# Sparse graph attention with residual and layer norm: the order of own and deep key blocks in a batch's last two tiles, and which engine weighs them

## The chip, the cores and the metric

The kernel runs on one core of a Trainium2 chip. The metric is the device time of one execution in microseconds (us). The engines are named as in the profile: PE is TensorE (PEld its weight loads), DVE is VectorE, ACT is ScalarE, POOL is GpSimd, SP is SyncE. POOL and SP also issue transfers (DMA).

## What is computed

One layer of multi-head attention on a graph, for 16 graphs of 1024 nodes with 512 features and 8 heads of 64, in float32, with a residual and a layer norm. The adjacency is one matrix for all 16 graphs. It is sparse and very uneven: the expected number of neighbours falls with the node's number.

```python
q = (x @ Wq + bq).reshape(b, n, H, HD)
k = (x @ Wk + bk).reshape(b, n, H, HD)
v = (x @ Wv + bv).reshape(b, n, H, HD)
scores = jnp.einsum('bqhd,bkhd->bhqk', q, k) / jnp.sqrt(jnp.float32(HD))
scores = scores + (1.0 - adj)[None, None, :, :] * -1000000000.0
attn = jax.nn.softmax(scores, axis=-1)
out = jnp.einsum('bhqk,bkhd->bqhd', attn, v).reshape(b, n, d)
return _layernorm(x + out @ Wo + bo)
```

## The kernel before

**Tiles and blocks.** The nodes are sorted by their number of neighbours and cut into 8 tiles of 128 queries. A batch (one graph) goes through its tiles in order. Only neighbours are computed: a block holds 128 pairs of a query and a key. In an own block i of a tile, each query of the tile meets its i-th neighbour. OWN (line 27) gives the number of own blocks by tile, 2, 1, 2, 3, 4, 5, 5, 7. Queries with more neighbours than that fill deep blocks, in which each of the 128 lines is a pair of any query of the tile with one more of its neighbours. BLOCKS (line 28) gives their number: one for tile 6, five for tile 7. Tile 1 needs no attention (one key), and tile 0 is done for the first two batches and then in the odd ones, for two batches together. This leaves 34 blocks in batches 0, 1 and the odd ones and 32 in the others, 530 in all.

**What a block does.** POOL gathers the keys' rows of k and v into a tile kvg (gather, line 1230, 512 KB), eight buffers in use (KG_BUFS); for a deep block it also gathers the rows of q into qg (line 1184, 256 KB). An own block uses the tile's q, loaded once by SP (line 1217). DVE multiplies q and k (products, line 1251) and sums by head (scores, line 1255), ACT takes the exponential (exponentials, line 1266). Then the rows of v are weighed by the exponentials (weigh): either ACT does it in eight small instructions, one for each head (line 1276), or DVE in one (line 1280). That frees the kvg buffer. An own block is then added by DVE to the tile's first block (add_own, line 1292; the first block itself, i = 0, needs no addition). A deep block is summed by PE into PSUM (add_up, lines 1301 and 1302), by a matrix that says which line belongs to which query. After the tile's last block, normalise (from line 1304) adds the two, divides, and hands the result to the output product.

**Which engine weighs.** by_act (line 1268) gives the own blocks other than the first to ACT. First and deep blocks go to ACT where the block's number n is even, to DVE where it is odd; in the first half batch all go to ACT, in the last batch all to DVE. Since every batch has an even number of blocks, the pattern is the same in each batch: of the six deep blocks, two go to ACT.

**Beside the blocks.** PE's main work is products: q, k and v of a batch ahead ("fronts"), by a scheme that computes k and v of two tiles together with seven products of sums (lines 947 to 979), and the output product po (line 790) of finished tiles, followed by the residual and the norm on DVE, ACT and POOL (complete, from line 1085) and a scattered store by POOL (line 1125). POOL also gathers x rows for the fronts (line 1001) and for the residual (line 1029).

**What sets the order.** All of it is written by hand: the loop from line 1470 takes one step for each block n, and each engine runs its instructions in the order in which they are issued there. In step n the exponentials of block n + 3 are issued, the products of n + 4, the gathers up to block n + 8, DVE's weighing of n + 1, the addition of own block n, the scores of n + 4, ACT's weighing of n + 2 and PE's sum of deep block n. A tile's normalise comes in the step of the next tile's first block. Between them PE's units of fronts and output products are issued by a credit, which grows in each step by a share of the batch's work. paced (line 1432) scales the share by load_of (line 1424), a guess of DVE's work in the step: 2, one more if DVE weighs block n + 1, one more for an own block that is not the first, and more for a tile's first block.

Of the kernel before, what the change touches and what calls it, by code (L numbers as in the profile page):

```python
# [26 lines left out]
OWN = (2, 1, 2, 3, 4, 5, 5, 7)  # L27
BLOCKS = (0, 0, 0, 0, 0, 0, 1, 5)
# [6 lines left out]
LONE, ONE_KEY, ONE_KEY_AT, ONE_KEY_LAST = 64, 1, (7, 4), (3, 0)  # L35
# [142 lines left out]
def kernel(  # L178
# [37 lines left out]
    B, N, D = x.shape  # L216
# [13 lines left out]
    own = [SHORT_KEYS * t for t in SHORT]  # L230
# [3 lines left out]
    NBT = NB - OWN[ONE_KEY]  # L234
# [19 lines left out]
    with ExitStack() as main:  # L254
# [82 lines left out]
        def merged(b):  # L337
            return b >= PAIRED_FROM and b % 2 == 1

        def tiles_of(b):  # L340
            return [t for t in range(NT) if t or b < PAIRED_FROM or merged(b)]
# [828 lines left out]


        KG, QG, PV, PSUM, QT, RDEN, V1 = {}, {}, {}, {}, {}, {}, {}
        blocks = [(b, t, i) for b in range(B) for t in tiles_of(b) if t != ONE_KEY for i in range(OWN[t] + BLOCKS[t])]
        start = [min(n for n, block in enumerate(blocks) if block[0] == b) for b in range(B)] + [len(blocks)]

        def load_more():
# [90 lines left out]

        def by_act(n):
            b, t, i = blocks[n]
            return 0 < i < OWN[t] or n < total - NBT and (n % 2 == 0 or n < NBT // 2)  # L1270

        def weigh(n):
            v, pv = KG.pop(n), PV[n]
            if by_act(n):
                for h in range(HEADS):
                    nc.scalar.activation(  # L1276
                        pv[:, ts(h, HD)], v[:, ds(D + h * HD, HD)], AF.Copy, scale=pv[:, D + h:D + h + 1]
                    )
                return
            nc.vector.tensor_tensor(  # L1280
                pv[:, 0:D].rearrange("p (h d) -> p h d", d=HD),
                v[:, D:].rearrange("p (h d) -> p h d", d=HD),
                pv[:, D:, None].to_broadcast([P, HEADS, HD]), op=OP.mult,
            )
# [134 lines left out]
        total = len(blocks)  # L1419
# [4 lines left out]
        def load_of(n):  # L1424

            b, t, i = blocks[n]
            had = 2.0 + (not by_act(min(n + 1, total - 1))) + (0 < i < OWN[t])
            if i == 0:
                had += 3.0 if BLOCKS[blocks[n - 1][1]] else 1.3
            return had  # L1430
# [17 lines left out]
        with tc.manual_schedule():  # L1448
# [20 lines left out]
            n = -LEAD_IN  # L1469
            while n < total or plan or rest or urgent or done or finishing or spilled or lone_tiles or not guarded:  # L1470
# [6 lines left out]
                elif n in start:  # L1477

                    b = start.index(n)
                    left = sum(u[0] for u in fronts)  # L1480
# [11 lines left out]
                if 0 <= n + 1 < total and not by_act(n + 1):  # L1492
                    weigh(n + 1)
# [96 lines left out]
```

## Time and profile before

| | |
|---|---|
| time, median of 3 runs | 1903.44 us (1902.83 to 1912.35) |
| the profiled execution's own time | 1892.33 us |
| its span, first to last instruction | 1890.4 us |
| mean granted clock of PE | 0.989 |
| ACT weighing, line 1276 | 3432 instructions, 864.6 us busy |
| DVE weighing, line 1280 | 101 instructions, median 0.683 us |
| DVE product, line 1251, and scores, line 1255 | 530 of each, 0.68 us each |
| DVE own addition, line 1292 | 329 instructions, mean 0.693 us |
| transfers | 544.63 MB, mean 288 GB/s |

How to read what follows. A row of a group or of a timeline names the line of the code, the engine, the operation, and what is written from what, with shapes as partitions x elements. In square brackets, or after the bar, stands the time for which the engine was idle just before, and what ended that. A row of the waits says which instruction waited for which, in total, how often, and the longest. A row of the stretches gives for each engine the busy time and the number of instructions, then the granted clock of PE (1 is full speed), the mean busy share of the 16 DMA engines, and GB/s. Engines run their instructions pipelined, so two instructions in a row can start less than one duration apart.

### The profile page before, as it was taken

The page shows a single profiled execution, that of the slowest core. Times are in us where ns is not written, and L with a number is a line of the kernel's source. Part 1 is how long each engine was busy: PE and PEld are TensorE (multiplying, and loading weights), DVE is VectorE, ACT ScalarE, POOL GpSimd, SP SyncE. Part 2 cuts the span into 40 slices and gives each one's busy share as a digit, 9 for nine tenths or more (in the row PEclk, how much of TensorE's full clock was granted, in tenths as well). Part 3 has the DMA queues.
Part 4 walks back from the last instruction along what each step waited for, and adds up shares of the span by engine and source line. Part 5 has one row for each costly group of instructions (what it writes and reads, how often), then busy time and mean ns, then how long its engine had stood idle before and what let it go on. Part 6 is the DMA issues. An engine that isn't in the chain of part 4 may idle for free. (4 is left out here: it accounts for less than half of the span.)

```text
span 1890.4 us, 25101 instructions
## 1 busy us (share of the span) xinstructions
PE 1815.1 (96%) x5149; PEld 878.2 (46%) x5149; DVE 1700.6 (90%) x3484; ACT 1531.7 (81%) x6016; POOL 1267.4 (67%) x1189
## 2 busy tenths in 40 slices
PE   7989999999999999999999999999999999999995
PEld 3434444444545454444445444444445444444442
DVE  6888889999999999899899989899999999997874
ACT  3627869979888988979798978989898989886794
POOL 1367766777677676757677676767666777656774
PEclk9989999999999999999999999999999999999997
DMA  7357787988889898888889898999889899989993
GB/s 280 114 168 226 233 307 227 315 295 294 308 287 316 305 328 283 305 288 307 312 292 335 271 334 274 314 304 310 301 307 326 293 356 310 314 277 340 334 319 117
DMA packets 188149, 544.63 MB, mean 288 GB/s; under 512 B 32602, under 2 KB 32622, under 8 KB 187986
## 3 DMA queue, kind: packets, MB, share of 16 engines
q0 software_dynamic: 116400, 382.82, 60.6%
q1 hardware_dynamic: 68510, 154.30, 21.8%
q10 hardware_dynamic: 3076, 5.82, 0.9%
q14 instruction: 120, 0.98, 0.2%
q8 instruction: 43, 0.70, 0.1%
HBM read 419.52 MB, written 144.34 MB: 298 GB/s over the span
## 5 line engine op out<-in xcount | busy, mean ns | idle before, releaser
L1276 ACT ACTIVATE pv<-kvg,pv 128x64 f32<-128x64 f32 x3432 | 864.6, 340 | 0.0
L1230 POOL DMA_INDIRECT kvg<-kv_pair,place_row x462 | 526.7, 1140 | 258.0 <-ACT pv L1276 73.3
L790 PE MATMUL po<-wo,oT 128*128 128x512 f32 x816 | 380.1, 596 | 1.0 <-ACT oT L1340 0.9
L790 PE MATMUL pq<-wq,xT 128*128 128x512 f32 x792 | 368.9, 597 | 0.4 <-DVE g L966 0.4
L1255 DVE TENSOR_REDUCE s<-qk 128x8 f32<-128x512 f32 x530 | 360.2, 680 | 7.5
L1251 DVE TENSOR_TENSOR qk<-qt,kvg 128x512 f32<-128x512 f32 x434 | 296.4, 683 | 22.2 <-DMA kvg<-kv_pair,place_row 22.1
L947 PE MATMUL pp<-t,s 128*128 128x512 f32 x504 | 237.4, 593 | 2.7 <-ACT sq_k L800 1.7
L947 PE MATMUL x<-b,xT 128*128 128x512 f32 x504 | 237.8, 594 | 0.8 <-ACT e L960 0.8
L790 PEld LDWEIGHTS po<-wo,oT 128*128 128x128 f32 x816 | 152.6, 191 | 166.8 <-issue 153.9
L1292 DVE TENSOR_TENSOR pv<-pv,pv 128x520 f32<-128x520 f32 x329 | 228.0, 693 | 0.7 <-ACT pv L1276 0.6
L790 PEld LDWEIGHTS pq<-wq,xT 128*128 128x128 f32 x792 | 149.2, 192 | 166.4 <-issue 155.0
L1266 ACT ACTIVATE pv<-s,absent 128x8 f32<-128x8 f32 x434 | 126.3, 293 | 79.8 <-DVE s L1255 76.2
L1001 POOL DMA_INDIRECT x<-in_x_dram,asked_row x120 | 130.2, 1085 | 88.3 <-PE pxT L748 40.5
L1125 POOL DMA_INDIRECT out_dram<-y,asked_row x129 | 144.8, 1122 | 35.7 <-issue 19.8
L800 ACT ACTIVATE sq_k<-kv 128x128 bf16<-128x128 f32 x512 | 150.9, 301 | 6.0 <-DVE kv L970 6.0
L947 PEld LDWEIGHTS pp<-t,s 128*128 128x128 f32 x504 | 94.2, 190 | 114.1 <-issue 101.4
L947 PEld LDWEIGHTS x<-b,xT 128*128 128x128 f32 x504 | 94.3, 191 | 111.5 <-issue 106.5
L1184 POOL DMA_INDIRECT qg<-q_rows,query_row x96 | 106.9, 1114 | 36.5 <-issue 24.7
L947 PE MATMUL z<-b,s 128*128 128x512 f32 x252 | 119.1, 595 | 6.5 <-DVE kv L975 6.5
L1029 POOL DMA_INDIRECT y<-in_x_dram,asked_row x93 | 104.5, 1124 | 27.5 <-issue 25.8
L947 PE MATMUL z<-t,s 128*128 128x512 f32 x252 | 120.0, 599 | 0.0
L947 PE MATMUL pp<-t,xT 128*128 128x512 f32 x252 | 118.4, 592 | 0.0
(276 smaller groups left out, 2766.7 us busy)
## 6 DMA issues: line engine op xcount, KB each, us to landing
kv_pair<-kv SPq DMA_DIRECT2D x98, 512.0 KB
q_rows<-q SPq DMA_DIRECT2D x106, 256.0 KB
qt<-q_rows SPq DMA_DIRECT2D x98, 256.0 KB
residual<-x SPq DMA_DIRECT2D x36, 256.0 KB
y<-residual SPq DMA_DIRECT2D x36, 256.0 KB
kv_rows<-kv SPq DMA_DIRECT2D x15, 512.0 KB
kvg<-kv_pair,place_row POOLq DMA_INDIRECT x462, 6.5
kv_pair<-kv SPq DMA_DIRECT2D x28, 256.0 KB
```

Of the source, the lines that this page charges most:

```text
L790: nc.tensor.matmul(p, lhs(c), w[:, c, :], start=(c == 0), stop=(c == NPAIR - 1))
L800: nc.scalar.activation(sq, s[:, ts(h, P)], AF.Square, scale=scale, accum_out=sums[:, h:h + 1])
L947: nc.tensor.matmul(R[bank], l[:, ts(c, P)], right[:, c, :], start=(first and c == 0), stop=(c == 1), skip_group_check=True,)
L1001: nc.gpsimd.indirect_dma_start(out=y, out_offset=None, in_=x_rows, in_offset=bass.IndirectOffsetOnAxis(ap=asked_row[:, t:t + 1], axis=0), ...
L1125: nc.gpsimd.indirect_dma_start(out=out_rows[b, t], out_offset=bass.IndirectOffsetOnAxis(ap=rows, axis=0), in_=y, in_offset=None, element_o ...
L1184: nc.gpsimd.indirect_dma_start(out=q, out_offset=None, in_=q_rows[b % ROWS], in_offset=bass.IndirectOffsetOnAxis(ap=rows, axis=0))
L1230: nc.gpsimd.indirect_dma_start(out=KG[n], out_offset=None, in_=rows, in_offset=bass.IndirectOffsetOnAxis(ap=(place_row if b else key_row)[ ...
L1251: nc.vector.tensor_tensor(QK[n], q, KG[n][:, 0:D], op=OP.mult)
L1255: nc.vector.tensor_reduce(S[n], QK.pop(n).rearrange("p (h d) -> p h d", d=HD), axis=AX.X, op=OP.add)
L1266: nc.scalar.activation(PV[n][:, D:], S.pop(n), AF.Exp, bias=bias)
L1276: nc.scalar.activation(pv[:, ts(h, HD)], v[:, ds(D + h * HD, HD)], AF.Copy, scale=pv[:, D + h:D + h + 1])
L1292: nc.vector.tensor_tensor(PV[b, t], PV[b, t], pv, op=OP.add)
```

## The change

In batches 1 to 15 the blocks of the tiles with deep blocks (6 and 7) come in another order. Tile 7 runs own 0, own 1, and then deep and own blocks in turn up to the last own block. Tile 6's only deep block comes after its third own block. Blocks keep their number i, and batch 0 keeps its order. Which engine weighs a deep block depends, from batch 1 on, on the parity of b + i and no longer on that of n. In odd batches this gives four of the six deep blocks to ACT, in even ones two. First blocks (i = 0) keep the parity of n, and the rules for the first half batch and for the last batch stay.

```diff
-        blocks = [(b, t, i) for b in range(B) for t in tiles_of(b) if t != ONE_KEY for i in range(OWN[t] + BLOCKS[t])]
+
+        def blocks_of(b, t):
+
+            own, deep = list(range(OWN[t])), list(range(OWN[t], OWN[t] + BLOCKS[t]))
+            if b == 0 or not deep:
+                return own + deep
+            spread = max(1, len(own) // (len(deep) + 1))
+            left = len(own) - spread * len(deep)
+            for j, i in enumerate(deep):
+                own.insert(left + j * (spread + 1), i)
+            return own
+
+        blocks = [(b, t, i) for b in range(B) for t in tiles_of(b) if t != ONE_KEY for i in blocks_of(b, t)]
...
         def by_act(n):
             b, t, i = blocks[n]
-            return 0 < i < OWN[t] or n < total - NBT and (n % 2 == 0 or n < NBT // 2)
+            if 0 < i < OWN[t]:
+                return True
+            turn_of = b + i if b and i else n
+            return n < total - NBT and (turn_of % 2 == 0 or n < NBT // 2)
```

## The prediction

> **What bounds the kernel now.** I read the page's first part, its groups, the waits by engine, stretches of 5 us, and the timelines around the longest PE waits. Part 1 and two of the groups:
>
> ```profile
> PE 1815.1 (96%) x5149; PEld 878.2 (46%) x5149; DVE 1700.6 (90%) x3484; ACT 1531.7 (81%) x6016; POOL 1267.4 (67%) x1189
> ...
> L1276 ACT ACTIVATE pv<-kvg,pv 128x64 f32<-128x64 f32 x3432 | 864.6, 340 | 0.0
> L1230 POOL DMA_INDIRECT kvg<-kv_pair,place_row x462 | 526.7, 1140 | 258.0 <-ACT pv L1276 73.3
> ```
>
> PE is the bound. To see whether its busy time is real I took start-to-start times from its timeline: a 128x512 f32 product is two records, 0.43 us apart, a transpose 0.108 us, one sum (L1301 and L1302) 0.87 us. Counted over the whole timeline this is about 1809 us of PE work in a span of 1890.4 us. The rest is some 25 us of start (to 140 us), 20 to 30 us of end (from 1845 us), and small holes between, of which those over 0.5 us sum to about 43 us. A change that touches no PE work can give back only holes. So I looked for what the largest holes wait for:
>
> ```profile
> POOL kvg L1230 <- ACT pv L1276: 88.0, 72, 6.2
> ...
> POOL kvg L1230 <- DVE pv L1280: 36.2, 16, 4.3
> ...
> DVE qk L1251 <- DMA kvg<-kv_pair,place_row: 25.6, 13, 4.9
> ...
> PE sum L1301 <- DVE pv L1280: 13.8, 6, 3.7
> ```
>
> The columns are total us, times, longest. Numbering the 530 products of L1251 in order gives each DVE wait a block: the waits for kvg of 4.28, 4.87, 4.24 and 2.93 us (804.9, 907.8, 1119.3, 1630.2 us) stand on the first blocks of batches 6, 7, 9 and 14, and nearly all of the 25.6 us lies between the last deep block of a tile 7 and the third tile of the next batch. Four PE waits before a sum follow from them: 3.75, 1.89, 2.82, 2.51 us. How the first comes about, POOL first:
>
> ```profile
> 776.00 0.95 POOL L1184 DMA_INDIRECT qg<-q_rows,query_row  x1 [0.30 <-issue]
> ...
> 790.21 1.01 POOL L1230 DMA_INDIRECT kvg<-kv_pair,place_row  x1 [0.30 <-ACT pv L1276]
> ...
> 796.55 1.01 POOL L1230 DMA_INDIRECT kvg<-kv_pair,place_row  x1 [0.30 <-ACT pv L1276]
> 797.86 1.01 POOL L1230 DMA_INDIRECT kvg<-kv_pair,place_row  x1 [0.31 <-ACT sq_k L800]
> ```
> ```profile
> 804.94 0.69 DVE L1251 TENSOR_TENSOR qk<-qt,kvg 128x512 f32<-128x512 f32 x1 [4.28 <-DMA kvg<-kv_pair,place_row]
> ```
> ```profile
> 806.29 1.22 PE L1301 MATMUL sum<-pv,sums 128*128 128x256 f32 x2 [3.75 <-DVE pv L1280]
> ```
>
> From 776.00 to 791.2 us POOL issues the five deep blocks' pairs of gathers (qg, kvg) and nothing else: 15.2 us, 3.0 us a block. Then come four other jobs, and only at 796.55 the first kvg of batch 6, whose product comes 8.4 us later. By its place in the program this gather belongs to step (7, position 4); DVE passed that step near 786 us. POOL is 10 us behind, then issues a kvg every 1.3 us, 524 KB each, and DMA fills:
>
> ```profile
> 800.00:805.00 5.00, 2.54 (x8) 1.14 (x6) 0.72 (x3) 2.12 (x9) 3.78 (x5) 1.00 1.02 412
> 805.00:810.00 5.00, 3.71 (x8) 2.47 (x9) 4.93 (x9) 2.06 (x9) 2.46 (x3) 0.66 0.97 349
> 905.00:910.00 5.00, 3.11 (x10) 1.48 (x9) 2.20 (x4) 0.47 (x2) 3.78 (x5) 1.00 1.03 400
> 1115.00:1120.00 5.00, 4.11 (x12) 1.90 (x10) 0.72 (x3) 0.00 (x0) 3.78 (x5) 1.00 1.02 411
> 1625.00:1630.00 5.00, 4.09 (x13) 2.10 (x12) 2.04 (x4) 4.06 (x19) 2.52 (x3) 1.00 1.04 411
> ```
>
> The last three columns are clock, DMA share, GB/s. In all four stalls DMA is full at 400 to 412 GB/s while DVE stands still; after the first, PE's clock is 0.66 for 5 us. ACT has its own pattern, summed from its timeline: idle 0 to 1 us in nearly every tile 6, 5% in the own blocks of tile 7, 12% in its deep blocks.
>
> [...]
>
> **The change part by part.** The sum is against the profiled execution: 1892.33 us, of which 1890.4 are span. The median shown is 1903.44, 11.1 more; I carry the difference over unchanged.
>
> (1) *Order of own and deep blocks, batches 1 to 15.* No instruction is added. Tile 7 becomes own 0, 1, then deep and own in turn, ending on an own block; tile 6's one deep block moves from sixth to fourth. DVE's product and reduction, ACT's exponential, both gathers and the sum move with the block. Gathers stay 8 steps ahead until the fronts are used up (7 or 8 for a batch's first block, before and after, worked from the planner's code). POOL: apart from block gathers it issues 129 stores, 120 x, 93 y and small powers, about 0.65 jobs a block at 1.3 us, 0.9 us. A deep block then costs 3.0 + 0.9 = 3.9 us against a pace of 3.33 us per deep block, so POOL falls back by some 3 us in five. Mixed, (5 x 3.0 + 7 x 1.3)/12 + 0.9 = 2.9 us, under the pace of 3.2. DMA: 544.6 MB less the kvg (530 x 0.524) and qg (96 x 0.262) leaves 242 MB, 128 GB/s. A deep run adds 0.786 MB/3.3 us = 238, together 366 GB/s, near the 400 where it is full; mixed, 0.633/3.2 = 198, together 326. Worth: the four PE waits (11.0 us), the shorter waits just behind them (about 4) and two clock dips (5 us at 0.66, and 5 us at 0.71 from 1630: 3.2) make 18. Lateness of POOL also comes from ACT's release of kvg buffers, which stays in part, so I take 60%: -11. Bounds -18 and 0.
>
> (2) *DVE work moved to ACT.* In each of the seven odd batches 1 to 13, four deep blocks instead of two are weighed by ACT; even ones keep two; the last batch keeps DVE. The instruction lists say the same: L1280 101 to 87, L1276 3432 to 3544. DVE: 14 x 0.60 us (start to start) = 8.4 us less. DVE is not the bound, but PE waits for it at pm, z, poT and pxT for some 13 us, half of that in odd batches. I take -2; bounds -7 and 0.
>
> (3) *The same on ACT.* Eight weighings are 1.93 us start to start (771.22 to 773.13 with nothing between), so 3.9 us more per odd batch, 27 in all, at nothing if ACT's idle time covers it. In tiles 6 and 7 of batches 3, 5, 7, 9, 11, 13 that idle time is 6.4, 8.6, 2.8, 4.3, 2.3 and 4.8 us: barely enough in two. Behind a late weighing stand ACT's copies out of PSUM, for which PE waits next, and the release of a kvg buffer, for which POOL waits. Taken +2; bounds 0 and 27.
>
> (4) *Pace of PE's units.* The weights of load_of now alternate (4 and 2 instead of 3 in own blocks), so PE's units come in turns of about 4 and 1 us per step. PE's queue is in order and full, so +1; bounds 0 and +4.
>
> (5) *Edges.* DVE waits 2.9 us in all for L1302 at normalise; the last deep block is now one step earlier, so that goes. At the very end the last block is an own one with ACT's 1.93 us before the add. But DVE waits there for PE's po until 1865.85, which covers it; and five qg are no longer in a row ahead of the 5.47 us wait for POOL at 1839.8. Taken -2; bounds -4 and +2. Tile 7's first sum comes five steps earlier into the single sum buffer, but still two steps after tile 6's normalise: nothing, at most 1.
>
> Sum: -11 - 2 + 2 + 1 - 2 = -12. 1892.3 - 12 = 1880.3 profiled; 1903.4 - 12 = 1891.
>
> **Rivals.** *The holes stay* (0.22). POOL's 124 us of waits for weighings (88.0 + 36.2) say buffers, not the pairs of gathers, make the first kvg late. Then (1) is 0, the rest -1: 1902. Against it: from 776 to 791 us POOL shows only issue gaps of 0.3.
> *ACT becomes the bound in odd batches* (0.16), ending slower: place, tiles 6 and 7 of odd batches; price, 3.9 us each; it decides once less than about half is covered by idle time. Half uncovered is 7 x 1.95 = 14, with +1 of (4) and (1) lost because the next batch's gathers wait on the late weighings, less 4 of (2) and (5): 1914. For it: the two batches with 2.8 and 2.3 us. Against it: any 13 blocks from tile 6 on hold at most 12 for ACT, as before.
> *All middle stalls go* (0.12): -18 - 7 - 4 + 1 = -28, 1875.
> That the change doesn't do what it says is excluded by the instruction lists.
>
> **How the numbers follow.** The forecast, 1891, has 0.50; its own range is 1884 to 1899. The range 1878 to 1908 leaves out about 0.08 of the large gain and 0.12 of the slow case. About 0.5%, 9.5 us, is what a measurement of this kernel can tell from no change. Faster: 0.38 of the forecast and all 0.12. Same: 0.12 of the forecast, 0.20 of the staying holes, 0.03 of the slow case. Slower: 0.13 and 0.02 of the holes.
>
> **What would show it.** Right: DVE's wait for kvg from kv_pair falls from 25.6 us to under 12, and PE's wait for L1280 before a sum in the middle from 11 to under 5; no 5 us at 400 GB/s with DVE under 3; DVE waits for L1302 near 0. Wrong: ACT idle near 0 through odd tiles 7 and waits of DVE or PE for L1276 of several us; or first blocks that still wait for kvg.

## The result and the profile after

| | before | changed | ratio, 95% interval |
|---|---|---|---|
| 16 runs of each: median (range) | 1909.95 us (1900.32 to 1919.07) | 1897.06 us (1890.87 to 1904.53) | 0.9928 (0.9910 to 0.9945) |
| later, another chip, 43 and 4 runs | 1890.40 us (1885.26 to 1900.41) | 1877.85 us (1876.78 to 1879.82) | 0.9943 (0.9923 to 0.9962) |

The changed kernel is faster by 0.6 to 0.7%. The forecast, 1891 over 1903.44, was a ratio of 0.9935. The medians of the same kernel differ by 20 us between the two groups of runs, so below times are compared only as ratios to the kernel before on the same chip, turned into microseconds by 1890 (in experiment 3 by 1927).

The page of the changed kernel, its first part and the two groups that were shown of the kernel before. Lines from 1230 on have moved: the gather of kvg is L1242, the product L1263, ACT's weighing L1291, DVE's L1295, the own addition L1307, the sums L1316 and L1317, the normalised output o L1337, its transpose L1351.

```profile
PE 1816.5 (96%) x5149; PEld 876.6 (46%) x5149; DVE 1695.3 (90%) x3470; ACT 1557.4 (82%) x6128; POOL 1262.6 (67%) x1189
...
L1291 ACT ACTIVATE pv<-kvg,pv 128x64 f32<-128x64 f32 x3544 | 893.4, 340 | 1.8 <-issue 1.8
L1242 POOL DMA_INDIRECT kvg<-kv_pair,place_row x462 | 522.6, 1131 | 258.6 <-issue 94.5
```

ACT has 112 instructions more and 25.7 us more busy time, DVE 14 fewer and 5.3 us less; PE's work is the same. This profiled execution spans 1892.4 us, that of before 1890.4. The latter (1892.33 us) is not one of the 16 runs above, and its DVE shows none of the pauses that no instruction explains ("issue"), which come to 22.5 us in the changed kernel's profile. So their spans can't be subtracted. The waits can be compared, as the second profiles below confirm. DVE's waits of the changed kernel (us in all, times, longest):

```profile
DVE qk L1263 <- DMA kvg<-kv_pair,place_row: 14.3, 13, 2.9
...
DVE pv L1307 <- ACT pv L1291: 8.0, 7, 1.8
```

and PE's:

```profile
PE z L947 <- DVE kv L975: 10.4, 5, 3.9
...
PE poT L1351 <- DVE o L1337: 6.9, 4, 2.5
...
PE sum L1316 <- DVE pv L1295: 4.1, 4, 1.9
```

DVE's wait for kvg fell from 25.6 to 14.3 us and its longest from 4.9 to 2.9. PE's wait for a weighing before a sum fell from 13.8 to 4.1. So far this is what step (1) said. But z, a product that waits for DVE's kv (L975), has come to the top of PE's list, and DVE now waits 8.0 us for ACT's weighings (0.6 before).

For a pair that can be subtracted, both kernels were run and profiled again on one chip, together with the two halves of the change.

### The profile page after: what moved, and what is told of

It reads as the page before. It is cut to its first block, busy times and chain, and to the rows that moved or that the text cites. A ratio compares the mean times of both kernels' runs of the same rounds, so it can differ in the third digit from the quotient of the medians.

```text
span 1892.4 us, 25171 instructions
## 1 busy us (share of the span) xinstructions
PE 1816.5 (96%) x5149; PEld 876.6 (46%) x5149; DVE 1695.3 (90%) x3470; ACT 1557.4 (82%) x6128; POOL 1262.6 (67%) x1189
## 5 line engine op out<-in xcount | busy, mean ns | idle before, releaser
L1291 ACT ACTIVATE pv<-kvg,pv 128x64 f32<-128x64 f32 x3544 | 893.4, 340 | 1.8 <-issue 1.8
L1242 POOL DMA_INDIRECT kvg<-kv_pair,place_row x462 | 522.6, 1131 | 258.6 <-issue 94.5
L1263 DVE TENSOR_TENSOR qk<-qt,kvg 128x512 f32<-128x512 f32 x434 | 296.8, 684 | 13.2 <-DMA kvg<-kv_pair,place_row 13.1
L1307 DVE TENSOR_TENSOR pv<-pv,pv 128x520 f32<-128x520 f32 x329 | 228.4, 694 | 8.2 <-ACT pv L1291 8.0
L947 PE MATMUL z<-b,s 128*128 128x512 f32 x252 | 121.4, 604 | 13.1 <-DVE kv L975 10.4
```

The lines of the kernel that those rows point to most:

```text
L947: nc.tensor.matmul(R[bank], l[:, ts(c, P)], right[:, c, :], start=(first and c == 0), stop=(c == 1), skip_group_check=True,)
L1242: nc.gpsimd.indirect_dma_start(out=KG[n], out_offset=None, in_=rows, in_offset=bass.IndirectOffsetOnAxis(ap=(place_row if b else key_row)[ ...
L1263: nc.vector.tensor_tensor(QK[n], q, KG[n][:, 0:D], op=OP.mult)
L1291: nc.scalar.activation(pv[:, ts(h, HD)], v[:, ds(D + h * HD, HD)], AF.Copy, scale=pv[:, D + h:D + h + 1])
L1307: nc.vector.tensor_tensor(PV[b, t], PV[b, t], pv, op=OP.add)
```

## Experiment 1: both kernels again, and each half alone

The kernel before, unchanged ("before_2"):

> The kernel before once more, unchanged, for a second profile: the one shown before belongs to an execution of 1892 us, 18 us under the median of 16. Both theories: time within 0.2% of before. If the late first gathers of a batch (spreading theory) are what the median execution pays for, this profile, at about 1905 us, shows DVE waiting for kvg from kv_pair for 30 to 45 us, not 25.6, and PE waiting before sums for 15 to 30 us. If the scatter has another source (clock, first batch), these stay at 26 and 14 us.

The changed kernel, unchanged ("after_2"):

> The changed kernel once more, unchanged, for a second profile. Both theories: 13 to 14 us under before. Spreading theory: DVE's wait for kvg from kv_pair is again near 14 us, about half of before's. Smoothing theory (the gain comes from ACT no longer falling behind in a row of own blocks): this wait is no smaller than before's when set beside the second profile of before, and ACT's waits for DVE and DVE's for ACT are.

The new order, with the old engine for each block ("order_alone", an edit to the changed kernel):

```diff
-            turn_of = b + i if b and i else n
+            turn_of = i if b and i else n
```

> The new order of blocks, with the blocks weighed by the engines that had them before (deep blocks 8 and 10 of tile 7 by ACT in every batch, tile 6's by DVE). Spreading theory: the order is what counts, -9 to -12 us of the 13.8, ratio 0.994 to 0.995. Rival, the split counts (DVE is the second busiest engine and is relieved of 14 weighings in odd batches): -3 us or less.

The new split in the old order ("split_alone", an edit to the kernel before):

```diff
-            return 0 < i < OWN[t] or n < total - NBT and (n % 2 == 0 or n < NBT // 2)
+            if 0 < i < OWN[t]:
+                return True
+            turn_of = b + i if b and i else n
+            return n < total - NBT and (turn_of % 2 == 0 or n < NBT // 2)
```

> The old order of blocks, with deep blocks from batch 1 on weighed by the parity of batch plus block number: in odd batches four by ACT instead of two. Spreading theory: between -3 and +3 us, since POOL's five pairs of gathers in a row stay. Rival, the split counts: -6 us or more.

| | ratio, 95% interval | DVE for kvg | PE for a sum's weighing | PE z for kv |
|---|---|---|---|---|
| before_2 | 0.9998 (0.9985 to 1.0010) | 26.4 us | 13.6 us | 6.2 us |
| order_alone | 0.9999 (0.9987 to 1.0010) | 15.7 | 4.2 | 15.5 |
| split_alone | 0.9953 (0.9936 to 0.9969) | 30.5 | 10.6 | 4.2 |
| after_2 | 0.9943 (0.9923 to 0.9962) | 16.1 | 4.9 | 8.0 |

This turns my account over. The new order shortens the waits for kvg and at the sums much as step (1) said, and by itself brings nothing that can be measured: between -2.5 and +1.9 us. The split, which I had put at -2 + 2 = 0, leaves the waits for kvg and most of those at the sums, and by itself brings 8.9 us (6 to 12). Order and split together can't be told from the split alone by these intervals. before_2 shows the same waits as the first profile of before, within about 1 us. Whether a longer execution has more of them wasn't tested, since this one took 1892.7 us, as the first had.

**Where the order's gain went.** The start of batch 14 shows it. In order_alone, DVE's timeline (start, duration, engine and line, and in brackets the idle time before) has:

```profile
1625.91 0.69 DVE L1263 TENSOR_TENSOR qk<-qt,kvg 128x512 f32<-128x512 f32 x1 [2.51 <-DMA kvg<-kv_pair,place_row]
1626.52 0.68 DVE L1295 TENSOR_TENSOR pv<-kvg,pv 128x512 f32<-128x512 f32 x1
1627.13 0.69 DVE L1307 TENSOR_TENSOR pv<-pv,pv 128x520 f32<-128x520 f32 x1
...
1629.85 0.68 DVE L975 TENSOR_TENSOR kv<-z,g 128x512 f32<-128x512 f32 x1
```

PE's timeline, and the two stretches of 5 us around it (PE, PEld, DVE, ACT, POOL with counts; clock, DMA share, GB/s):

```profile
1630.59 2.08 PE L947 MATMUL z<-b,s 128*128 128x512 f32 x2 [5.14 <-DVE kv L975]
```
```profile
1625.00:1630.00 5.00, 0.45 (x2) 0.00 (x0) 4.05 (x10) 5.00 (x22) 3.33 (x4) 0.96 1.01 396
1630.00:1635.00 5.00, 4.41 (x6) 2.19 (x7) 3.01 (x5) 4.33 (x22) 3.78 (x5) 0.50 0.95 371
```

The product still waits 2.51 us for kvg with DMA near full. Behind it in DVE's queue stand a weighing, an own addition, the scores and five small operations, four of them for the products of x, and only then the kv that PE's next product needs. PE does nothing for 5.14 us and then runs at a clock of 0.50. In before_2, kv L975 ran at 1627.12, ahead of the product that waits. Here PE's wait has thus moved from the sum to the next result that PE takes from DVE. That kv now stands behind the product can come from the pace: load_of sees the new order, so order_alone also deals PE's units out to other steps. The two were not separated. Two more long waits for kv appear in order_alone, 3.85 us at 1082.1 and 3.50 at 1194.6; the first is in both profiles of the changed kernel too (3.86 each time), the other two aren't. These two are no returned waits for kvg: in the 10 us before each of them DVE didn't wait for kvg, but had other work ahead of kv, and before_2 already has 2.36 us at the place of the second.

DMA was not relieved either. Of the 342 stretches of 5 us from 140 to 1850 us, DMA moved at least 395 GB/s in 28 of before_2, 30 of split_alone, 34 of the first profile of the changed kernel, and 45 of order_alone and of after_2. In step (1) I had worked out 326 GB/s for a mixed run instead of 366, and had taken the full stretches to go. What went is the long DVE stall inside them.

**What the split does.** The same place in before_2, DVE, PE, and the stretch:

```profile
1630.30 0.69 DVE L1251 TENSOR_TENSOR qk<-qt,kvg 128x512 f32<-128x512 f32 x1 [2.50 <-DMA kvg<-kv_pair,place_row]
1630.91 0.68 DVE L1280 TENSOR_TENSOR pv<-kvg,pv 128x512 f32<-128x512 f32 x1
```
```profile
1631.65 0.70 PE L1301 MATMUL sum<-pv,sums 128*128 128x256 f32 x2 [2.33 <-DVE pv L1280]
```
```profile
1625.00:1630.00 5.00, 4.32 (x14) 2.30 (x13) 2.04 (x4) 4.27 (x20) 3.01 (x3) 1.00 1.04 413
```

and in split_alone, DVE and the stretch:

```profile
1628.08 0.70 DVE L1251 TENSOR_TENSOR qk<-qt,kvg 128x512 f32<-128x512 f32 x1 [3.87 <-DMA kvg<-kv_pair,place_row]
1628.81 0.69 DVE L1255 TENSOR_REDUCE s<-qk 128x8 f32<-128x512 f32 x1
```
```profile
1625.00:1630.00 5.00, 5.00 (x17) 3.04 (x16) 1.89 (x5) 3.18 (x19) 3.45 (x5) 1.00 1.03 417
```

In split_alone DVE waits longer for the same kvg, 3.87 us, and DMA is as full; yet PE is busy for the whole 5 us. The step that issues the product of a batch's first block (n + 4) issues DVE's weighing of block n + 1, which is deep block (7, 9) of the batch before. In the kernel before that weighing stands right behind the product that waits, and PE's sum waits for it. After an odd batch the new split gives (7, 9) to ACT, and the sum doesn't see DVE's stall. Only a few batch starts show such waits. Sums after odd batches (to batches 6 and 14) waited 3.30 + 2.33 = 5.6 us in before_2 and 1.1 in split_alone. Those after even batches, where (7, 9) stays on DVE, waited 5.1 us in before_2 and 6.7 in split_alone. So this wait shrank by 4.5 us, less 1.6 given back after even batches: 2.9 of the 8.9 us. The rest I couldn't pin on one wait.

## Experiment 2: amounts or places

Four edits to the kernel before, run on another chip than experiment 1; the kernel before took 1890.95 us there. "dve_more": in the odd batches 1 to 13, blocks (6, 5) and (7, 9) are weighed twice by DVE, so 14 weighings or 8.4 us more (0.60 us each from start to start).

```diff
-            nc.vector.tensor_tensor(
+            b, t, i = blocks[n]
+            for _ in range(2 if b % 2 and b < B - 1 and (t, i) in ((6, 5), (7, 9)) else 1):
+                nc.vector.tensor_tensor(
...
```

> The kernel before, with two deep blocks of each of the seven odd batches (tile 6's and the third of tile 7, both DVE's) weighed twice by DVE: 14 x 0.60 = 8.4 us more on DVE, nothing else changed, ACT and the pace of PE's units included. Theory now (PE waits for DVE at whatever stands next in its queue, so DVE's work in the tiles of the blocks is paid for one to one): +7 to +10 us, ratio 1.004 to 1.005. Rival, place (the split pays because the last deep block of an odd batch no longer stands behind DVE's product that waits for kvg): 0 to +3. The forecast's own step, that DVE is not the bound and 8.4 us of it are worth 2: +2.

"act_more": in the same batches ACT weighs (7, 8) and (7, 10) twice, 27 us more (14 weighings of 1.93 us).

```diff
-                for h in range(HEADS):
+                b, t, i = blocks[n]
+                for h in [*range(HEADS)] * (2 if b % 2 and b < B - 1 and (t, i) in ((7, 8), (7, 10)) else 1):
```

> The kernel before, with the two deep blocks that ACT weighs in each of the seven odd batches weighed twice by ACT: 14 x 1.93 = 27 us more on ACT, nothing else changed. Theory now: ACT has room, 0 to +3 us. Rival of the forecast, ACT becomes the bound in odd batches: +10 or more. With dve_more it tells what the two halves of the split are worth one by one.

"swap_last": in those batches ACT takes (7, 9) and (7, 11) in place of (7, 8) and (7, 10); the amounts stay.

```diff
-            return 0 < i < OWN[t] or n < total - NBT and (n % 2 == 0 or n < NBT // 2)
+            if 0 < i < OWN[t]:
+                return True
+            if 0 < b < B - 1 and b % 2 and i:
+                return (t, i) in ((7, 9), (7, 11))
+            return n < total - NBT and (n % 2 == 0 or n < NBT // 2)
```

> The kernel before, with ACT weighing the third and the last deep block of tile 7 in odd batches in place of the second and the fourth: as much work on each engine as before, but the last deep block no longer queued on DVE behind the next batch's products. Theory now (amount of DVE's work): -2 to +2 us. Rival, place: -5 us or more.

"split_all": split_alone with the odd batches' pattern in the even ones too, `turn_of = i + 1`. ACT then has four of six deep blocks in every batch from 1 to 14.

> The old order of blocks, with four of six deep blocks weighed by ACT in the even batches 2 to 14 as well: 28 weighings moved from DVE to ACT instead of 14. Theory now: twice the gain of the split, -14 to -18 us against before, as long as ACT's idle time covers 3.9 us per batch. Rival, ACT becomes the bound, or the gain of the split was one of place in odd batches: no more than the split's -9.

| | ratio, 95% interval | in us |
|---|---|---|
| dve_more | 1.0022 (1.0009 to 1.0035) | +4.2 (1.7 to 6.6) for 8.4 us of DVE |
| act_more | 1.0022 (1.0007 to 1.0037) | +4.2 (1.3 to 7.0) for 27 us of ACT |
| swap_last | 0.9966 (0.9951 to 0.9981) | -6.4 (-9.3 to -3.6) for nothing in the amounts |
| split_all | 1.0029 (1.0018 to 1.0040) | +5.5 (3.4 to 7.6) |

DVE's added work is paid by about half, ACT's by about 15%. For dve_more this is less than the +7 to +10 that I expected by then. It is no pure test of the amount either: half of its added weighings are those of (7, 9), in the very place described above, and the sums waited 16.9 us in it instead of 13.6. If work taken away gives what added work costs, which no run tests, the change's amounts come to -4.2 + 4.2 = 0. That is what my -2 + 2 said, with each term about half of what is measured here. So the amounts, as far as these two runs show them, are not what made the split pay. Swapping which two blocks ACT weighs, with no change of amounts, gives 6.4 us, beside split_alone's 8.9 on the other chip. In swap_last's trace the sums after odd batches waited 2.6 us instead of 5.6, those after even ones 6.4 instead of 5.1. The direction is the same as in split_alone, but the net of the two is 1.7 us of the 6.4. So the runs show that this wait moves as described, and not that it makes the gain. swap_last, split_alone and split_all also change what by_act tells load_of, and so the places of PE's units; experiment 3 comes back to that.

In split_all new waits lead. PE's waits there:

```profile
PE z L947 <- DVE kv L975: 12.8, 7, 4.7
PE x L947 <- ACT e L960: 7.1, 2, 4.8
...
PE sum L1304 <- DVE pv L1283: 3.3, 4, 1.7
```

The sums wait 3.3 us only, but PE waits 12.8 us for kv and 7.1 for ACT. Measured against the kernel before on each chip, split_all is some 14 us worse than split_alone. The 7.1 us, of which 4.8 lie in one wait behind ACT's weighings in batch 12, are what the rival "ACT becomes the bound" said. The waits for kv are not: before the two longest, 4.09 us at 439.3 and 4.74 at 663.3, DVE had other work of its own directly ahead of kv. So the rival is real in part, and how much of the 14 us is its doing stays open. In the odd batches alone it shows as DVE's wait for ACT's weighings (0.6 us before, 7.4 and 8.0 after) and doesn't decide.

**A second measure.** PE's work is the same in all these kernels, so I added up PE's busy time times granted clock over the stretches from 140 to 1740 us, which leaves out the start and the last batch. That this product is work done is an estimate. The records of z in order_alone fit it: the four from 1630.59 us on, of which two are shown above, took 3.78 us at a clock of 0.50, four of the same form at 437.72 took 1.98 at 1.00. before_2 had done 1562.7 us of it, after_2 10.0 more, split_alone 4.9 more, swap_last 3.8 more, order_alone 1.0 less, act_more 3.5, split_all 5.7 and dve_more 7.7 less. The signs agree with the measured ratios, and so does the order but for dve_more. The first profile of the changed kernel, the one with the pauses, doesn't fit: it had done 1.4 us less than before_2. PE's idle time in the same stretch is 32.4 us in before_2, 32.6 in order_alone, 29.1 in split_alone and 23.3 in after_2. Single profiles also differ at the end, where the code is the same. Near its last products before_2 ran PE at:

```profile
1860.00:1865.00 5.00, 5.00 (x11) 2.17 (x11) 0.27 (x1) 0.68 (x1) 3.02 (x4) 0.71 0.51 190
...
1870.00:1875.00 5.00, 4.53 (x6) 1.96 (x7) 0.98 (x5) 1.93 (x3) 2.55 (x3) 0.50 0.43 164
```

By the same estimate, clock below 1 cost 6.1 us there after 1830 (busy time times what the clock lacks to 1), 4.5 in the first profile of before, 1.6 in after_2, 1.5 in split_alone, 1.6 in dve_more, 4.6 in act_more, 6.2 in swap_last and nothing in split_all, with the last batch the same in all but after_2. So of the 16.2 us between the spans of before_2 and after_2, some 4.5 are the end's clock by this estimate.

## Experiment 3: the pace, and the gathers of q

These four ran on yet another chip, on which the kernel before took 1927.48 us.

"pace_alone": the kernel before, whose load_of alone is told the new split.

```diff
...
-            had = 2.0 + (not by_act(min(n + 1, total - 1))) + (0 < i < OWN[t])
+            had = 2.0 + (not paced_act(min(n + 1, total - 1))) + (0 < i < OWN[t])
```

> The kernel before, with every block in its place and weighed by the engine that weighed it before; only load_of, by which PE's units are dealt out to the steps, is told the changed split of the deep blocks. Planner theory (the split pays because it moves PE's units, one output product unit from the last batch to the one before among them): -5 to -9 us. Engine theory (it pays because DVE's queue is shorter or has the last deep block no more): -2 to +2.

"split_old_pace": split_alone, whose load_of is told the old split, by the same line. All weighings are as in split_alone, and PE's units are dealt out as before.

> The old order of blocks with the changed split, load_of still told the old one, so that PE's units stand where they stood before. Planner theory: -2 to +2 us. Engine theory: -6 to -9, as split_alone.

"after_flat_pace": the changed kernel with one weight for all blocks of tiles 6 and 7 but the first.

```diff
+            if BLOCKS[t] and i:
+                had = 3.0
```

> The changed kernel, with load_of giving every block after the first of tiles 6 and 7 the same weight, 3, so that PE's units no longer come in turns of 4 and 1 us. If the uneven pace is what eats the gain of the new order: 4 to 10 us under the changed kernel, so 15 to 20 under before. If a stall taken away at a sum comes back at the next result of DVE that PE needs, whatever the pace: within 3 us of the changed kernel, about -10 against before.

"no_qg": the kernel before without the 96 gathers of q; deep blocks multiply with the tile's own q, so their scores are others, with as much work on DVE, ACT and PE.

```diff
-                tag, bufs = ("qt", Q_BUFS) if fronts or i % 2 else ("xT", 4)
-                QG[n] = work.tile([P, D], F32, tag=tag, name=f"qg_{n}", bufs=bufs)
-                gather_q(QG[n], b, (query_row if b else query_row0)[:, g:g + 1])
...
-            if i < OWN[t]:
-                q = QT[b, t] if i < OWN[t] - 1 else QT.pop((b, t))
-            else:
-                q = QG.pop(n)
+            q = QT[b, t] if n + 1 < total and blocks[n + 1][:2] == (b, t) else QT.pop((b, t))
```

> The kernel before, leaving out the 96 gathers of queries for deep blocks (it uses the tile's own queries there, so deep scores are those of other pairs): POOL has 96 jobs of 1.4 us fewer, DMA 25 MB less, five in a row per batch. The forecast's step, POOL and DMA fall behind there and make the next batch's first kvg late: DVE's wait for kvg falls from 26 to under 8 us and the time by 11 to 18. Theory now (PE and DVE are both nearly full and in order, so a wait for kvg that goes comes back as one of DVE for PE or of PE for the next result of DVE): the wait falls, the time by 5 us or less.

| | ratio, 95% interval |
|---|---|
| pace_alone | 0.9996 (0.9974 to 1.0019) |
| split_old_pace | 1.0013 (0.9986 to 1.0041) |
| after_flat_pace | 0.9972 (0.9953 to 0.9990) |
| no_qg | 0.9735 (0.9700 to 0.9770) |

The split's pace told alone costs nothing within 5 us. split_old_pace shows no gain: its interval, -2.7 to +7.9 us, leaves out the -6 to -9 that I expected if the split acts through DVE's queue alone. It fits what I had written for the other case, that the split pays only together with its own pace. But split_alone was not run on this chip, so chip and pace are not separated, and the point stays open. It weakens the account by place: in swap_last, too, the pace went with the place. after_flat_pace is faster than before by 0.28%, some 5 us, less than either of the two cases that I had named; the changed kernel was not run there, so nothing says whether its pace helps or hurts. No version was shown to beat the changed kernel.

no_qg is the plain miss. I had expected 5 us or less and measured 51 on this chip. Some of that may be the chip's pauses (last section), of which no_qg has fewer. Its runs, 1872 to 1878 us, are 12 to 18 us below what the kernel before took on the chip of experiment 1 (1890), where such pauses are absent. DVE's wait for kvg in its profile:

```profile
DVE qk L1245 <- DMA kvg<-kv_pair,place_row: 0.5, 1, 0.5
```

Without the second gather of each pair the waits for kvg are gone. POOL's idle time before the gathers of kvg from kv_pair, where the rival "the holes stay" looked for the cause, is longer there: 328.5 us, of which 109.6 ended with ACT's weighings, against 258.0 and 73.3 in the first profile of before. So the premise of step (1) holds: the pairs make the first kvg late. Whether they do so by POOL's time or by DMA's bytes, no_qg doesn't separate, since it takes away both. What they cost is larger than my 5 us, and by the 12 to 18 us may be what step (1) had put on it (18 at most); the 51 can't be told from the pauses. Spreading the pairs doesn't collect it.

## Why the prediction was right in number and wrong in its sum

- **Step (1), -11 for the order: the step that failed.** What it said of the waits was right: 25.6 to 14.3 us for kvg, 13.8 to 4.1 for the sums, no wait for kvg of 4 us left. That DMA would be relieved was wrong (45 full stretches against 28). Its price was wrong, 0 (-2.5 to +1.9) in place of -11. (A small part was a slip: the two clock dips counted 3.2 us, though PE was busy for only 3.71 and 3.40 of their 5 us, which makes 2.2. That the dips would go with the waits was an estimate; in after_2 the clock was 0.58 in the stretch in which z's wait of 3.86 us for kv ended.) I priced the waits that go and asked too little what is late next: PE's waits on z for kv came to 15.5 us in order_alone against 6.2, about as much more as the sums lost (9.4). At batch 14 kv stands further back in the same delayed DVE queue; the other two long waits come from where PE's units and DVE's other work now stand.
- **Steps (2) and (3), -2 and +2 for the split.** The net of the amounts, 0, fits dve_more and act_more (4.2 and 4.2), if taking away gives what adding costs. But the split is worth -8.9. swap_last shows with equal amounts that it matters which weighings are moved, together with the pace that goes with them; I had treated all 14 alike. A wait that accounts for it is seen for 2.9 of the 8.9 us, the one at the sums. Whether the rest needs the split's pace is open (split_old_pace).
- **Step (4), +1 for the pace.** pace_alone tells load_of only the new split, not the new order: -0.8 (-5.0 to +3.7). That is no contradiction, but the pace of the whole change was not run alone.
- **Step (5), -2 at the edges.** DVE's wait for L1302 at normalise went from 2.9 us to 0.5 for L1317. The end itself varies by up to 6 us with the clock (the estimates above: nothing in split_all, 6.2 us in swap_last), so its worth was not resolved.
- **What would show it.** Two of four signs came as written: the sums' waits in the middle fell to 1.1 us (after_2) and DVE's waits for L1302 to near 0. DVE's wait for kvg fell to 14.3 and 16.1 us, not under 12. Stretches with DMA at 400 GB/s or more and DVE under 3 of 5 us came in one profile and not in the other: five in both profiles of before, none in the first of the changed kernel, three in after_2 (from 140 to 1850 us). One sign of the wrong case came too, DVE's waits of 7.4 and 8.0 us for ACT's weighings, and didn't decide.
- **Rivals.** "The holes stay" was wrong on the kvg waits, but right for the order's worth in time. "ACT becomes the bound" came true only in split_all, and there in part.

So -12 was forecast and -11 to -14 came, by luck: two errors cancel, and the 11 us put on the order belong to the split, or to the two together. Order and split might be worth more together than the sum: after_2 had done 10.0 us more of PE's work by 1740, the two alone -1.0 and +4.9, and its wait of z for kv is 8.0 us, not order_alone's 15.5. But the first profile of the changed kernel waits 10.4 us on z for kv and has no such lead, and the measured ratios don't resolve it.

## What to carry to other kernels

Here PE and DVE were 96% and 90% busy, what stood behind a late instruction in DVE's queue was late with it (at batch 14 of order_alone kv started 3.94 us after the product that had waited), and as much waiting as left the sums came up at other results that PE takes from DVE. In such a kernel, price a removed stall by what stands behind it in the late engine's queue, not by its length alone. When work is moved between engines, ask also which instruction then no longer stands behind a wait; moving equal amounts in another place was worth 6.4 us here. An edit that goes through a planner moves other work too: keep the plan fixed in a test, on the same chip as the test that it is set beside. Run an edit's halves alone before believing which half works: here the half that changed the traced waits most changed the time least.

## What the runs showed that I had not expected

- The same kernel before had medians of 1909.95, 1890.4, 1890.95 and 1927.48 us in the four groups of runs, of which the last three were on three different chips. In the profiles on the slowest of these chips, several engines show extra pauses of 2 to 5 us that no instruction explains ("issue"; in pace_alone the longest are 5.3 us on PE and 5.5 on DVE), and batch 0, the same code in the kernels compared, took 145 us instead of 133. no_qg, on that chip, also has a long batch 0 (142 us), but less of the pauses: PE shows 3.2 us of them against 14 to 16 in the other three. The first profile of the changed kernel has some too, with 139 us for batch 0. Why was not found.
- Waits reproduce far better than times: two profiles of the kernel before put 25.6 and 26.4 us on kvg and 13.8 and 13.6 on the sums, and the 3.86 us wait of batch 8 in the changed kernel came out the same in both of its profiles. With the pauses of the slowest chip this no longer holds: pace_alone has 18.6 us on kvg.
- In order_alone PE was idle for 5.14 us and ran at a clock of 0.50 in the next stretch, in which it was busy for 4.41 us. By these figures the low clock cost PE about 2.2 us beside the wait itself, an estimate. The four records of z took 3.78 us there, and also after the wait of 3.86 us in after_2 (2.61 in the first profile of the changed kernel); 2.46 us after the 3.85 us and 1.98 after the 3.50 us in order_alone, no more than after 0.53 us. What sets the clock was not shown.
